# Two sets of row-wise Mamba blocks in one sequence of steps, and the layer's input added in the second

## The chip, the cores and the metric

The kernel runs on one core of a Trainium2 chip. The metric is device time in microseconds (us), from the first to the last instruction of one launch; lower is better. Eight runs of the kernel before gave 20162.97 to 20181.85 us, median 20176.18.

## What is computed

Four layers follow each other on a batch of four images of 48 x 48 pixels and 192 channels (the kernel holds an image as channels x 2304 pixels). Layers 0 to 2 are not touched by the change. Layer 3 normalizes its input `x`, runs a bidirectional Mamba block along each column of pixels (weights `mv`) and another along each row (weights `mh`), joins them with a linear layer, adds the input, and ends with a normalized two-layer MLP:

```python
xn = _layernorm(x, ln1_g, ln1_b)
h = _mamba_bidir(xn.reshape(B * H, W, C), ph).reshape(B, H, W, 2 * C)
xv = jnp.swapaxes(xn, 1, 2).reshape(B * W, H, C)
v = jnp.swapaxes(_mamba_bidir(xv, pv).reshape(B, W, H, 2 * C), 1, 2)
u = jnp.concatenate([v, h], -1)
x = x + jnp.einsum('bhwe,oe->bhwo', u, fc_w) + fc_b
xn2 = _layernorm(x, ln2_g, ln2_b)
m = jax.nn.gelu(jnp.einsum('bhwc,ec->bhwe', xn2, mlp_w1) + mlp_b1, approximate=False)
return x + jnp.einsum('bhwc,oc->bhwo', m, mlp_w2) + mlp_b2
```

One `_mamba` projects its input to `xi` and `z` (384 channels each), convolves `xi` over 4 pixels of the line, derives from it a step width `dt` and 16 pairs of coefficients B and C per pixel, and scans along the line, for each channel and each of 16 states: `h = exp(dt * A) * h + dt * x * B`. The output is the sum over the states of `h * C`, plus `D * xc`, times `silu(z)`, projected back to 192 channels.

## The kernel before

All data are float32. Layer 3 is three calls at the end of `network`: `row_mambas` for `mv` on the turned images `xn_wh`, `row_mambas` for `mh` on `xn_hw`, and `mlp`. The linear layer that joins the directions is folded into the weights beforehand: for each direction `row_mambas` multiplies `wo` (the Mamba block's own output projection) with a part of `fc` on PE, twice three products with two operand pairs each (tile `fp`, L1375 to L1380), and ACT copies them to `outT`. What remains for the end is `x3 + fc_b + f[1] + turned(f[0])`, where `f[0]` and `f[1]` are the outputs of the two sets in DRAM and `x3` is the layer's input.

**Jobs and groups.** A job is one direction of one piece of 384 pixels (eight lines of 48). There are 4 images x 6 pieces x 2 directions = 48 jobs in a set; the two directions of a piece are a pair, and the second (the *twin*) shares the input `u`, its projection `xh` and the gate `z` with the first. In a job, three blocks of 128 channels (index i) and four groups of four states (index g) make 12 groups. `run_jobs` goes through all groups of all jobs, one step each, and writes out by hand, for each step, what goes to which engine:

- DVE: the product `inputs` = `du` x B (into PSUM), then the scan `h`, always in program order (class `InOrder`).
- ACT: the decays `a` = exp(dt A) of the group two steps ahead, the copies out of PSUM, and the Silu and Softplus of later jobs, in a fixed order.
- POOL: the product `h` x C of the step's group (`weigh`), and, by step, a gate `yt` x `z` (steps 2, 6, 10 of a job) or a product `dus` (steps 1, 5, 9) behind it, all in program order.
- PE: the sum over states by matmuls of `h` with the identity into `y` (`reduce`, one step later), and the projections and convolutions of the next job.
- SP: all DMAs. A scheduler of the framework sets their order. B and C go to DRAM (`bc`) and come back broadcast to all partitions (`bcb`, 1536 KB per group of states, five buffers).

The work of the next job is a list of *units* (a PE part and an ACT part with the steps in which they may be issued), handed out by `Stream`. `MambaJob.outputs` gives two more units, which project a finished pair's `yt` with `outT` into `o` in steps 7 and 9 of the next pair's first job; after the second the store `f<-o` is issued. When a set ends, `run_jobs` first drains the pipeline, and when one begins, it loads a first job, projects and convolves it, and forms its first decays, all before the first group.

**Weights.** `MambaWeights` (L817) loads `xpT`, `dtT`, `vec` and `inT` and forms `A`, `diagD` and `diag` on ACT and DVE. `row_mambas` makes it once for each set, in a pool that is released at the end of the set.

**The MLP** (`mlp`, L1393) first loads its weights, then `pre(b)` loads three whole images (`macc` from `x3`, two `mf` from `f`; 1728 KB each) and adds them on DVE: two `scalar_tensor_tensor` (L1429), each on 96 x 2304, and two `tensor_tensor` with a turned operand (L1433). Six pieces per image then go through nine software-pipelined stages: mean, center, square, variance, root, scale, affine, hidden, close. Three buffers differ in number: `macc` has two, each `mf` one.

Of the kernel before, what the change touches and what calls it, by code (L numbers as in the profile page):

```python
# [14 lines left out]
ALU = mybir.AluOpType  # L15
PSUM = bass.MemoryType.PSUM

B = 4
S = 48
L = S * S  # L20
# [13 lines left out]
def halves(d):  # L34

    return d.rearrange("(k p) l -> p k l", p=Q)
# [11 lines left out]
class InOrder:  # L48


    def __init__(self, tc, engine):
        self.tc, self.engine = tc, engine
# [235 lines left out]
class ScanJob:  # L288
# [2 lines left out]

    def __init__(self, k, pools, w, c0, rev, prev):
        self.k, self.pools, self.w, self.c0, self.rev, self.prev = k, pools, w, c0, rev, prev
        self.entry, self.tokens = pools.entry(rev)
        self.bcb = {}
        self.y = {}
        self.a = {}
        self.h = {}  # L300
        self.du = {}
# [191 lines left out]
class MambaJob(ScanJob):  # L493

    skips = True

    def __init__(self, k, pools, w, c0, rev, prev, src, dst, mirror=False, twin=None):  # L500
        super().__init__(k, pools, w, c0, rev, prev)
        self.src, self.dst, self.mirror, self.twin = src, dst, mirror, twin
        self.paired = False
        if twin is not None:
            twin.paired = True
# [35 lines left out]
    def units(self, last):  # L541
# [40 lines left out]

        if self.twin is not None:
            self.z = self.twin.z
            outputs = last.outputs((7, 7), (9, 9)) if last is not None else []
            bc, deltas = self.projections(lambda: self.xs, (3, 3), (5, 5))
            return [conv(0, 0, 0), conv(1, 1, 2), conv(2, 2, 2), bc, *deltas, *outputs]
        outputs = last.outputs((4, 4), (6, 6)) if last is not None else []
        bc, deltas = self.projections(lambda: self.xs, (5, 5), (7, 7))
        return [  # L590
            inner(0, 0, 0),
# [2 lines left out]
            *(conv(i, min(2 + i, 3), 3) for i in range(3)),  # L594
            *outputs[:1],
            bc,
            *outputs[1:],
            *deltas,
            gate(0, 9, 10),
            gate(1, 10, 10),  # L600
            gate(2, 10, 10),
# [15 lines left out]
    def outputs(self, *slots):  # L617
        k = self.k
        if self.paired:
            return []  # L620
        step = -1 if self.mirror else 1
        jobs = [self] if self.twin is None else [self.twin, self]

        def project(m, slots):
            def act(ps):
                if m == 0:
                    self.o = k.tile(self.pools.one, [Q, 2, CH], "o")
                k.copy(self.o[:, m, ::step], ps)
                if m == 1:
                    d0 = L - CH - self.c0 if self.mirror else self.c0  # L630
                    k.nc.sync.dma_start(halves(self.dst)[:, :, d0 : d0 + CH], self.o)

            return self.unit(
                slots,
                Q,
                lambda ps: (
                    ps,
                    [
                        (job.w.outT[:, i, m * Q : (m + 1) * Q], job.yt[:, i, :])
                        for job in jobs  # L640
                        for i in range(3)
                    ],
                ),
                act,
            )

        return [project(m, slots[m]) for m in range(2)]


class Stream:  # L650
# [62 lines left out]
def run_jobs(jobs, side=None):  # L713
# [29 lines left out]
    for t in range(len(groups) + gated):  # L743
# [6 lines left out]
        if at == per - ahead:  # L750
            stream.run(at - 1)
        if at == taken + 3 and n + 1 == len(jobs) and n:
            Stream(jobs[n - 1].outputs((0, 0), (0, 0))).run(per)
        if t < len(groups):
            job, i, g = groups[t]
            job.scan(i, g)
# [6 lines left out]
        if t < len(groups):  # L763
# [3 lines left out]
            job, i, g = groups[t]  # L767
            job.weigh(i, g)
        stream.run(at if at < per - 1 else per)
        if side is not None and t < len(groups):  # L770
            if at == taken + 1 and n:
                offer(jobs[n - 1])
            side.slot(at)
            side.end()
# [4 lines left out]
        if 0 <= t - behind < len(groups):  # L779
            job, i, g = groups[t - behind]  # L780
            job.reduce(i, g)
    Stream(jobs[-1].outputs((0, 0), (0, 0))).run(per)
    offer(jobs[-1])


# [31 lines left out]
class MambaWeights(Weights):  # L817
    def __init__(self, k, pool, inT, xpT, dtT, vec, tag):
        super().__init__(k, pool, 128, 12, xpT, dtT, vec, tag)
        nc = k.nc  # L820
        self.D = self.vec[:, :, 17:18]
        self.cb = self.vec[:, :, 18:19]
        self.diagD = k.tile(pool, [128, 3, 128], f"diagD{tag}")
# [2 lines left out]
                self.diagD[:, i, :], k.ident, self.D[:, i, :], None, ALU.mult  # L826
            )
        self.taps = vec.shape[1] - 19
        self.inT = k.tile(pool, [Q, 2, 768], f"inT{tag}")
        nc.sync.dma_start(self.inT, inT.rearrange("(k p) m -> p k m", p=Q))  # L830
        self.diag = k.tile(pool, [128, 3, self.taps, 128], f"diag{tag}")
        for i in range(3):
            for t in range(self.taps):
                nc.vector.tensor_scalar(
                    self.diag[:, i, t, :],
                    k.ident,
                    self.vec[:, i, 19 + t : 20 + t],
                    None,
                    ALU.mult,
                )  # L840


def mamba_pass(k, pools, w, rev, src, dst, mirror=False):
# [18 lines left out]
def mamba_pair(k, weights, srcs, outs, mirror):  # L862

    with ExitStack() as ctx:
        pool = ctx.enter_context(k.tc.tile_pool(name="w", bufs=1))
        ws = []
        for n, (inT, xpT, dtT, vec, outT) in enumerate(weights):
            w = MambaWeights(k, pool, inT, xpT, dtT, vec, f"_{n}")
            w.outT = k.tile(pool, [128, 3, C], f"outT_{n}")
            k.nc.sync.dma_start(w.outT, outT.rearrange("(k p) m -> p k m", p=128))  # L870
            ws.append(w)
# [485 lines left out]
    return begin  # L1357


def row_mambas(k, weights, fcT, srcs, outs):  # L1360


    with ExitStack() as ctx:
        pool = ctx.enter_context(k.tc.tile_pool(name="w", bufs=1))
        inT, xpT, dtT, vec, wout = weights
        w = MambaWeights(k, pool, inT, xpT, dtT, vec, "")
        ws = [w, copy(w)]
        wo = k.tile(pool, [Q, 2, 2 * C], "wo")
        k.nc.sync.dma_start(wo, wout.rearrange("(k p) m -> p k m", p=Q))
        fc = k.tile(pool, [Q, 2, 2, C], "fc")  # L1370
        for n in range(2):
            k.nc.sync.dma_start(fc[:, n, :, :], fcT[n].rearrange("(k p) m -> p k m", p=Q))

        outT = [k.tile(pool, [128, 3, C], f"outT_{n}") for n in range(2)]
        with k.tc.tile_pool(name="fp", bufs=2, space=PSUM) as fp:  # L1375
            for n in range(2):
                for i in range(3):
                    p = k.tile(fp, [128, C], "fp")
                    k.mm(p, [(wo[:, m, i * 128 : (i + 1) * 128], fc[:, n, m, :]) for m in range(2)])
                    k.copy(outT[n][:, i, :], p)  # L1380
        pools = ScanPools(k, ctx, 1, True)
        jobs = []
        for n in range(2):
            ws[n].outT = outT[n]
        for b in range(B):
            for c in range(NCH):
                of = None, srcs[b], outs[b]
                first = MambaJob(k, pools, ws[0], c * CH, False, *of)
                jobs += [first, MambaJob(k, pools, ws[1], c * CH, True, *of, twin=first)]
        run_jobs(jobs)  # L1390


def mlp(k, f, fcb, ln2, w1T, b1, w2T, b2, x3, out):  # L1393

    nc, tc = k.nc, k.tc

# [2 lines left out]
    with (  # L1399
# [3 lines left out]
        tc.tile_pool(name="fout", bufs=2, space=PSUM) as po,  # L1403
        tc.tile_pool(name="fl", bufs=3, space=PSUM) as lnps,
    ):
        w1 = k.tile(one, [Q, 2, 3 * C], "mw1")
        nc.sync.dma_start(w1, w1T.rearrange("(k p) m -> p k m", p=Q))
        w2 = k.tile(one, [128, len(blocks), C], "mw2")
# [4 lines left out]
            nc.sync.dma_start(b1t[:n, e : e + 1], b1[at].rearrange("(p v) -> p v", v=1))  # L1413
        b2t = k.tile(one, [Q, 2], "mb2")
        nc.sync.dma_start(b2t, b2.rearrange("(k p) -> p k", p=Q))
        nw = k.tile(one, [Q, 2, 3], "mnw")
        nc.sync.dma_start(nw[:, :, 0:2], ln2.rearrange("(k p) v -> p k v", p=Q))
        nc.sync.dma_start(nw[:, :, 2:3], fcb.rearrange("(k p v) -> p k v", p=Q, v=1))
        acc, xn, hid = {}, {}, {}

        def pre(b):
            acc[b] = k.tile(pool, [Q, 2, L], "macc")
            nc.sync.dma_start(acc[b], halves(x3[b]))
            y = []
            for n in (1, 0):
                y.append(k.tile(one, [Q, 2, L], f"mf{n}"))
                nc.sync.dma_start(y[-1], halves(f[n][b]))
            for m in range(2):
                nc.vector.scalar_tensor_tensor(  # L1429
                    acc[b][:, m, :], acc[b][:, m, :], nw[:, m, 2:3], y[0][:, m, :], ALU.add, ALU.add  # L1430
                )
            for m in range(2):
                nc.vector.tensor_tensor(  # L1433
                    square(acc[b][:, m, :]),
                    square(acc[b][:, m, :]),
                    flipped(y[1][:, m, :]),
                    ALU.add,
                )

        def chunk(b, c):  # L1440
            return acc[b][:, :, c * CH : (c + 1) * CH]
# [30 lines left out]
def network(tc, d, out):  # L1472
    with ExitStack() as ctx:
# [44 lines left out]


        f = [images("f") for _ in range(2)]  # L1520
        for n, (p, src) in enumerate((("mv", xn[1]), ("mh", xn[0]))):
            ws = tuple(d[f"L3_{p}_{v}"] for v in ("inT", "xpT", "dtT", "vec", "Wout"))
            fcT = [d["L3_fcT"][2 * n + i] for i in range(2)]
            row_mambas(k, ws, fcT, src, f[n])
        mlp(k, f, *(d[f"L3_{v}"] for v in ("fc_b", "ln2", "w1T", "b1", "w2T", "b2")), x3, out)

# [114 lines left out]
```

## Time and profile before

| | us |
|---|---|
| median of 8 runs | 20176.18 |
| the profiled execution | 20172.9 |
| its span, first to last instruction | 20171.1 |
| first set: first product to end of last scan | 13525.79 to 16582.52 |
| second set: the same | 16638.98 to 19699.61 |
| MLP: first matmul to last operation | 19754.33 to 20167.2 |

| engine | busy, us | share of the span |
|---|---|---|
| PE | 17590.7 | 87% |
| DVE | 18228.2 | 90% |
| ACT | 12814.8 | 64% |
| POOL | 14692.9 | 73% |

The profile names an instruction by engine, line and the tiles it writes and reads (`out<-in`). A line can be a helper's: L56 stands for all operations that `InOrder` passes on, L93 for ACT, L114 for matmuls, so groups are told apart by their tiles. In the lines of a timeline, the first two numbers are the start and the duration in us, `x` gives how many instructions are merged into the row, and brackets hold the engine's idle time before it and what ended it. `SPq` rows are DMA issues, not transfers. In a table of stretches, each row has the stretch, its length, then busy time and count for PE, weight loads (PEld), DVE, ACT and POOL, then the granted TensorE clock (1.00 is full), the DMA engines' mean share, and GB/s.

### The profile page before, as it was taken

How to read it: one execution, taken by the hardware profiler on the slowest of the kernel's cores; microseconds unless marked ns; L12 is line 12 of the kernel's file. 1: busy time of each engine (PE TensorE's matmuls, PEld its weight loads, DVE VectorE, ACT ScalarE, POOL GpSimd, SP SyncE). 2: the span in 40 equal slices, each digit the busy share in tenths (PEclk: the TensorE clock that was granted, in tenths of full speed). 3: DMA queues.
4: the chain of work that ended last, by engine and by line, in shares of the span. 5: the costliest groups of instructions: out<-in, count | busy, mean ns of one | idle time of the engine just before them, and what ended most of it. 6: DMA issues, size and time to landing. Idle time of an engine off the chain costs nothing.

```text
span 20171.1 us, 159086 instructions
## 1 busy us (share of the span) xinstructions
PE 17590.7 (87%) x48144; PEld 8291.9 (41%) x48144; DVE 18228.2 (90%) x7435; ACT 12814.8 (64%) x22448; POOL 14692.9 (73%) x10748
## 2 busy tenths in 40 slices
PE   8999996999997778888888888879998988989988
PEld 4444443444444322233333333334444444444444
DVE  8999997999998499999999999969999989999993
ACT  6666664666665366666666766656666656666663
POOL 7777775777777177888877878757777767777770
PEclk9999998999999889989999999989999999999999
DMA  3323334333333266666666666642322222222222
GB/s 115 108 104 110 108 110 116 111 111 105 107 107 110 74 129 142 139 148 146 141 146 144 141 139 134 144 112 106 106 106 106 103 94 104 103 105 106 104 103 59
DMA packets 476473, 2320.46 MB, mean 115 GB/s; under 512 B 74553, under 2 KB 313761, under 8 KB 315105
## 3 DMA queue, kind: packets, MB, share of 16 engines
q1 hardware_dynamic: 475616, 2310.29, 40.7%
q8 instruction: 386, 6.32, 0.1%
q14 instruction: 471, 3.85, 0.1%
HBM read 2110.68 MB, written 199.40 MB: 115 GB/s over the span
## 4 chain that ended last, share of the span: by engine, by line
POOL 37%; DVE 35%; issue 11%; PE 11%; ACT 3%; DMA 3%; SPq 0%; DVEq 0%; POOLq 0%; ACTq 0%
POOL h L56 29%; DVE h L56 22%; DVE inputs L56 11%; PE y L56 5%; PE ps L56 3%; POOL dus L56 3%; POOL state L56 2%; POOL yt L56 1%; PE vps L114 1%; DMA bcb<-bc 1%; ACT a L93 1%; POOL bcb L56 1%; PE mop L114 1%; PE mps L114 1%; DVE vxi L1030 1%
## 5 line engine op out<-in xcount | busy, mean ns | idle before, releaser
L56 POOL TENSOR_TENSOR h<-h,bcb 128x1536 f32<-128x1536 f32 x3456 | 11914.4, 3447 | 1764.7 <-DVE h L56 1490.0
L56 DVE TENSOR_TENSOR_SCAN h<-a,inputs 128x1540 f32<-128x1540 f32 (+1 forms) x3456 | 11610.4, 3359 | 449.1 <-ACT a L93 12.7
L93 ACT ACTIVATE a<-delta,A 128x384 f32<-128x384 f32 (+1 forms) x13824 | 7447.9, 604 | 3369.5 <-DVE h L56 3357.7
L56 PE MATMUL y<-h,ident 128*128 128x384 f32 x18432 | 6806.7, 517 | 583.5 <-POOL h L56 578.4
L56 DVE TENSOR_TENSOR inputs<-du,bcb 128x1540 f32<-128x1540 f32 (+1 forms) x3456 | 6115.4, 1770 | 560.0 <-ACT du L93 206.6
L56 PEld LDWEIGHTS y<-h,ident 128*128 128x128 f32 x18432 | 3622.7, 201 | 3625.0 <-POOL h L56 1096.4
L56 PE MATMUL y<-h,sum 128*64 128x384 f32 x9216 | 3683.6, 549 | 577.0 <-POOL h L56 471.5
L56 PEld LDWEIGHTS y<-h,sum 128*64 128x64 f32 x9216 | 1297.8, 151 | 2921.7 <-issue 1758.7
L56 POOL COPY state<-h 128x4 f32<-128x4 f32 x2304 | 434.0, 188 | 2384.2 <-DVE h L56 2365.9
L56 PE MATMUL ps<-xh,diag 128*128 128x384 f32 x4032 | 1419.0, 491 | 196.1 <-ACT xc L93 196.1
L56 PE MATMUL ps<-u,inT 96*128 96x384 f32 x3456 | 1261.4, 496 | 198.8 <-ACT z L93 133.6
L56 PE MATMUL ps<-bcd,dtT 12*128 12x384 f32 (+1 forms) x2304 | 1022.3, 551 | 383.4 <-ACT delta L93 379.3
L56 PEld LDWEIGHTS ps<-xh,diag 128*128 128x128 f32 x4032 | 750.8, 189 | 790.3 <-ACT xc L93 282.9
L93 ACT ACT_TABLE_LOAD x793 | 1017.4, 1283 | 13.9
L90 ACT ACT_TABLE_LOAD x785 | 1007.2, 1283 | 14.1 <-PEq L1633 0.7
L56 PEld LDWEIGHTS ps<-u,inT 96*128 96x128 f32 x3456 | 651.3, 192 | 711.6 <-ACT z L93 210.7
L93 ACT ACTIVATE delta<-ps,vec 128x384 f32<-128x384 f32 x1152 | 632.9, 579 | 327.4 <-PE ps L56 320.0
L56 PE MATMUL ps<-yt,outT 128*96 128x384 f32 x2304 | 789.5, 486 | 0.7 <-POOL yt L56 0.7
L56 PEld LDWEIGHTS ps<-bcd,dtT 12*128 12x128 f32 (+1 forms) x2304 | 384.1, 192 | 953.2 <-ACT delta L93 616.7
L56 POOL TENSOR_TENSOR dus<-delta,xc 128x384 f32<-128x384 f32 x576 | 575.6, 999 | 139.6 <-ACT delta L93 139.6
L93 ACT ACTIVATE du<-dus 128x384 f32<-128x384 f32 x1152 | 560.5, 487 | 158.6 <-DVE inputs L56 153.0
L56 POOL TENSOR_TENSOR dus<-delta,xs 128x384 f32<-128x384 f32 x576 | 575.1, 999 | 56.0 <-ACT delta L93 56.0
(132 smaller groups left out, 9310.0 us busy)
## 6 DMA issues: line engine op xcount, KB each, us to landing
bcb<-bc SPq DMA_DIRECT2D x384, 1540.0 KB
bcb<-bc SPq DMA_DIRECT2D x768, 770.0 KB
bcb<-bc SPq DMA_DIRECT2D x384, 1536.0 KB
y<-o SPq DMA_DIRECT2D x192, 288.0 KB
xs<-xi_wh SPq DMA_DIRECT2D x96, 288.0 KB
xs<-xi_hw SPq DMA_DIRECT2D x96, 288.0 KB
added<-y SPq DMA_DIRECT2D x96, 288.0 KB
xs<-x_wh SPq DMA_DIRECT2D x96, 288.0 KB
```

What stands on the lines that cost most here:

```text
L56: return lambda *a, **kw: self.tc.keep_in_program_order(op(*a, **kw))
L90: self.in_order(self.nc.scalar.preload_act_table_set(LOG_EXP))
L93: return self.in_order(self.nc.scalar.activation(out, in_, func, **kw))
L114: (engine or self.nc.tensor).matmul(out, lhsT, rhs, start=start and i == 0, stop=stop and i == n - 1)
L1030: nc.vector.scalar_tensor_tensor(acc, taps, v[:, i, 1 + t : 2 + t], acc, ALU.mult, ALU.add)
```

## The change

Both sets become one list of jobs, and one call of `run_jobs`. `row_mambas` takes a list of sets; it makes the weights of both at the start, and the folds of both, with `wo` and `fc` in a pool that is released after them. Only `inT` keeps one buffer for both sets: a new method `enter` loads it, for the first set at once, for the second in step 1 of the first set's last-but-one job (`extras`, run by `run_jobs` after the step's units). The jobs of the second set get `prior`, the image of `x3`: their `outputs` have two more units, in steps 10 and 11, without a PE part, which add a loaded piece of `x3` to `o` on POOL, and the store follows the second of these.

In `mlp`, `x3` is no longer loaded. `load(b)` fetches `f[0][b]` into `mf` and `f[1][b]` into `macc` by halves (864 KB each) and adds both and the bias in one `scalar_tensor_tensor` per half, with `f[0]` read turned. `load(0)` stands ahead of the weights, and `pre(b)` calls `load(b + 1)`. `mf` now has two buffers. In the other user of `MambaWeights`, `mamba_pair`, `enter` is called right after the weights are made.

```diff
 # MambaJob.units
-            outputs = last.outputs((7, 7), (9, 9)) if last is not None else []
+            outputs = last.outputs((7, 7), (9, 9), (10, 10), (11, 11)) if last is not None else []
 # MambaJob.outputs
+        def add(m):
+            k.g.tensor_tensor(self.o[:, m, :], self.o[:, m, :], prior[:, m, :], ALU.add)
+            if m == 1:
+                store()
...
-                if m == 1:
-                    d0 = L - CH - self.c0 if self.mirror else self.c0
-                    k.nc.sync.dma_start(halves(self.dst)[:, :, d0 : d0 + CH], self.o)
+                if m == 1 and self.prior is None:
+                    store()
...
+        if self.prior is not None:
+            prior = k.tile(self.pools.one, [Q, 2, CH], "prior")
+            k.nc.sync.dma_start(prior, halves(self.prior)[:, :, d0 : d0 + CH])
+            units += [(slots[2 + m], lambda: None, lambda m=m: add(m)) for m in range(2)]
 # run_jobs
+        if t < len(groups):
+            for slot, extra in jobs[n].extras:
+                if slot == at:
+                    extra()
 # MambaWeights
+    def enter(self, tag="inT"):
+        self.inT = self.k.tile(self.pool, [Q, 2, 768], tag)
+        self.k.nc.sync.dma_start(self.inT, self.in_src.rearrange("(k p) m -> p k m", p=Q))
 # row_mambas
+        for (there, back), (*_, srcs, outs, prior) in zip(pairs, sets):
+            if jobs:
+                jobs[-2].extras = [(1, there.enter)]
+            else:
+                there.enter()
+            for b in range(B):
+                for c in range(NCH):
+                    of = None, srcs[b], outs[b]
+                    last = prior[b] if prior is not None else None
+                    first = MambaJob(k, pools, there, c * CH, False, *of)
+                    jobs += [
+                        first,
+                        MambaJob(k, pools, back, c * CH, True, *of, twin=first, prior=last),
+                    ]
         run_jobs(jobs)
 # mlp
+        def load(b):
+            acc[b] = k.tile(pool, [Q, 2, L], "macc")
+            y = k.tile(pool, [Q, 2, L], "mf")
+            for m in range(2):
+                nc.sync.dma_start(y[:, m, :], f[0][b][m * Q : (m + 1) * Q, :])
+                nc.sync.dma_start(acc[b][:, m, :], f[1][b][m * Q : (m + 1) * Q, :])
+                nc.vector.scalar_tensor_tensor(
+                    square(acc[b][:, m, :]),
+                    square(acc[b][:, m, :]),
+                    nw[:, m, 2:3],
+                    flipped(y[:, m, :]),
+                    ALU.add,
+                    ALU.add,
+                )
+
+        load(0)
...
         def pre(b):
-            acc[b] = k.tile(pool, [Q, 2, L], "macc")
-            nc.sync.dma_start(acc[b], halves(x3[b]))
-            y = []
-            for n in (1, 0):
-                y.append(k.tile(one, [Q, 2, L], f"mf{n}"))
-                nc.sync.dma_start(y[-1], halves(f[n][b]))
...
+            if b + 1 < B:
+                load(b + 1)
```

In the SP queue of the changed program, as the scheduler orders it: at the start, `xpT`, `dtT` and `vec` of both sets, `wo` and `fc` of both, then `inT`. In each pair of the second set, four `bcb` fetches, the store of `f`, the load of `prior`, and the next `bc` (in the first set, as before, the store stands ahead of the fourth `bcb`). At the end, the last store of `f`, `w1`, the first image's four halves, the other weights, the second image's halves.

## The prediction

> **What bounds the kernel now.** I read the page's activity slices first, then the busy time of each engine in the three stretches that the change touches, then the order of events at their seams.
>
> ```profile
> DVE  8999997999998499999999999969999989999993
> POOL 7777775777777177888877878757777767777770
> 13525.80:16582.50 3056.70, 2742.57 (x7679) 1450.79 (x7678) 2949.67 (x1152) 1964.43 (x3386) 2276.81 (x1140) 0.94 0.29 104
> 16638.90:19699.60 3060.70, 2745.68 (x7679) 1453.49 (x7678) 2949.68 (x1152) 1964.94 (x3387) 2277.26 (x1140) 0.94 0.29 103
> 19754.30:20166.50 412.20, 402.76 (x1152) 184.79 (x1152) 138.46 (x156) 182.48 (x259) 0.00 (x0) 0.99 0.22 52
> ```
>
> The first two lines are two rows of the 40 slices; the others give busy time by stretch (PE, weight loads, DVE, ACT, POOL, then clock, DMA share, GB/s). The first two stretches are the two sets of layer 3 blocks, from the first DVE product to the last scan: DVE is busy 96% of each, POOL 74%, DMA 29%. So in the sets DVE decides, with 576 groups in 3056.7 and 3060.7 us, 5.31 us a group. The last stretch is the MLP: PE is busy 402.8 of 412.2 us and decides, DVE a third. Between the stretches lie seams in which neither bounds anything. The first, by the timeline of DVE:
>
> ```profile
> 16579.17 3.35 DVE L56 TENSOR_TENSOR_SCAN h<-a,inputs 128x1536 f32<-128x1536 f32 x1
> 16600.17 0.06 DVE L249 MEMSET ones<- 128x1 f32 x1 [17.65 <-DMA f<-o]
> ...
> 16638.98 1.77 DVE L56 TENSOR_TENSOR inputs<-du,bcb 128x1536 f32<-128x1536 f32 x1 [34.87 <-ACT du L93]
> ```
>
> The last scan of the first set ends at 16582.52 and the next product begins at 16638.98: 56.46 us, in which the first set drains (17.65 us idle, then weights), and the second loads weights, folds `outT`, projects, convolves and forms its first decays. The seam to the MLP, seen from PE:
>
> ```profile
> 19714.30 0.33 SPq L631 DMA_DIRECT2D f<-o  x1
> 19717.02 0.33 SPq L1407 DMA_DIRECT2D mw<-in_L_w1T  x1
> ...
> 19742.42 5.14 DVE L1429 SCALAR_TENSOR_TENSOR macc<-macc,mnw,mf 96x2304 f32<-96x2304 f32 x2 [42.81 <-DMA mf<-f]
> 19750.18 8.03 DVE L1433 TENSOR_TENSOR macc<-macc,mf 96x2304 f32<-96x2304 f32 x2 [2.61 <-DMA mf<-f]
> 19754.33 2.84 PE L114 MATMUL ln_ps<-macc,mean 96*96 96x384 f32 x4 [40.58 <-DVE macc L1433]
> 19758.27 2.88 PE L114 MATMUL ln_ps<-macc,mean 96*96 96x384 f32 x4 [1.09 <-DVE macc L1433]
> ```
>
> **1. The merged sequence removes the first seam.** The boundary becomes an ordinary pair of jobs: the new set's projections and convolutions run beside the old set's last scans, as every pair's do. All 56.4 us go from DVE's path. The one new load there, `inT` (576 KB), is issued ahead of the last pair's `u`; in the pair shown at 18041, `u` is issued 66 us before its projection runs on PE at 18107.7. Even behind the old buffer's last reader that is cover enough. If it weren't, the span from first projection to first product (16613.34 to 16638.98, 25.6 us) would stay. Gain 56.4, bounds 30.8 and 56.4.
>
> **2. The same work at the start of the first set.** The second set's weights and folds now stand before the first set.
>
> ```profile
> 13495.86 6.06 PE L114 MATMUL fp<-fc,wo 96*128 96x192 f32 x24 [37.15 <-DMA fc<-in_L_fcT]
> 13497.52 0.33 ACT L93 ACTIVATE outT<-fp 128x192 f32<-128x192 f32 x1 [7.30 <-PE fp L114]
> ```
>
> Five more DMAs are issued before `wo` at 0.4 to 0.5 us each, and `inT` moves behind them (-0.5): PE starts about 2 us later. Six more fold groups follow on PE; the six of before took 5.9 us, three at 1.28 and, once the clock was up, three at 0.65. Six warm ones cost 3.9, cold ones 7.7. `inT`, last in the queue, is issued near 13494.7 and isn't read before 13507. The second set's 15 `diag` scalings on DVE (3.1 us, from the rows at 16601) lie under the wait for `fc`. All else follows the folds in order, so nothing hides this: +6.3 us (2.2 + 4.1), bounds 5.6 and 10.
>
> **3. The added input.** Per pair of the second set: one 288 KB load, and two POOL adds of 96x384. This shape has a row in another stage:
>
> ```profile
> 13424.42 0.99 POOL L56 TENSOR_TENSOR nx<-nx,nrs 96x384 f32<-96x384 f32 x1 [56.77 <-ACT nrs L93]
> ```
>
> So 48 x 0.99 = 48 us of POOL, in a queue that idles a quarter of the stage. By place: the first add stands in step 10 behind the `h` product and ahead of the `yt` gate, the second behind `h` of step 11. In the pair at 18101, `h` (3.41 from start to next), gate (0.94) and memset (0.15) end at 18106.02, and DVE releases the next `h` at 18106.73; with the add POOL is ready at 18107.03, 0.3 us late. Step 11 then ends with its add, the `xh` and `a` memsets near 18112.0, when the next release is due at 18112.07. The lag is gone within one step. Queued behind the adds are the gate (its product is read 8 steps on), the memset of the decay buffer (scanned two steps on, 10 us) and `h` (four buffers, read by PE one step on). DVE waits for none of them at once: cost 0; without cover up to 48.
>
> On SP the store of `f` now waits for the second add, about 12 us later than at present, and the load of `prior` follows it. In the first set, one broadcast fetch `bcb` stands behind the store; in the second, all four stand ahead of it, and behind it only the next `bc` store, which waits for ACT's `bcd` another 26 us (18112 to 18138). `prior` has one buffer, but is asked for right after it was read and used some 20 steps later. Cost 0; 24 x 288 KB is 2% of the stage's traffic.
>
> *By the Trainium skill*, "GPSIMD Engine Reference", section 4.1, elementwise two-input work belongs on VectorE, since GpSimd is about 2x slower; the rows here agree (0.95 us for DVE's 96x768 `ln_xm`, 0.99 for half of it on POOL). Followed, it would put 48 x 0.47 = 23 us on the engine that bounds this stage; the sum below stays with POOL at 0.
>
> **4. The MLP's start.** The image's sum now needs two loads instead of three and two DVE passes instead of four, in halves of 864 KB. At present the two first 1728 KB loads take 18.1 us from the first issue (19724.35) to the first pass, the third 7.76 more; so 1728 KB are worth 10.3 us in front and 7.76 after. The last store is 1.1 us later (one add on POOL, the other is under PE): 19715.4. The image's load is issued as `mw` is now, 2.7 later: 19718.1. First halves land at 19728.4, second halves at 19736.2. The fused pass, with the turned operand, isn't in the trace: its neighbours are the unturned one (2.61) and the turned add (4.10), both of 96x2304; it can't well be worse than the two it replaces (6.7). I take 4.1, as the turned read sets the row's length: second half done at 19740.3 against 19758.2 (when PE's fourth wait ends). That is 18; 1 us off for `mw`, which shares the queue: gain 17, bounds 13 and 20. The other weights stand behind these loads, but `w1` is ahead of them and `w2` isn't needed before the eighth stage of the first chunk, 20 us on.
>
> **5. The MLP's other images.** PE waits for L1433 at three more places: 0.64 + 1.86, 1.30 + 1.19, 1.36 + 1.20 = 7.55 us. A burst of 13.3 us on DVE becomes two passes of 4.1, asked for earlier. I take 4, bounds 0 and 7.5. Fewer DVE cycles elsewhere are worth nothing: PE bounds.
>
> **Sum**, from the profiled execution (20172.9, its span 20171.1): -56.4 + 6.3 + 0 - 17 - 4 = -71.1, 20101.8. The median of the runs is 3.3 above the profiled one: 20105.
>
> **Rivals**, on the median's scale.
> - *The adds cost what they take.* If `h`'s 0.3 us lag doesn't end within a step, but POOL's extra 2 us of each pair reach DVE: +48, 20153. Against it: POOL's 26% idle and the four `h` buffers. For it: step 11 closes with under 0.1 us to spare.
> - *The seam stays in part.* A new wait (for `inT`, or the new set's first `delta`) takes its place: +25.6, 20131. Against: 66 us of cover.
> - *The MLP doesn't start earlier*, because the loads are bound by DMA or a later weight replaces them: +21, 20126. For it: the first image's and the weights' bytes share one queue, and each DMA waits for an earlier one's semaphore.
> - *Slower than before.* The store on SP waits for POOL, and the next `bc` and its fetches queue behind store and `prior`. From 26 us of lateness on, each further microsecond is lost in each of 24 pairs; from 29 us it eats the gain (71/24 = 3 us a pair); at 31, 20105 + 24 x 5 = 20225. It needs `prior` to land over 100 us late; nothing in a queue at 29% shows that.
>
> **Chances**: forecast 0.70 (its own range 20088 to 20118, from the bounds of 2, 4 and 5), MLP unchanged 0.08, seam in part 0.07, adds 0.10, slower 0.05. The range 20085 to 20136 takes in the first three and leaves out the last two. A change under 0.2%, about 40 us, can't be told from none here: forecast, MLP and seam are faster (0.85), the adds' case is within 0.2% (0.10), the last slower (0.05).
>
> **What would show it.** DVE: no gap above 1 us at the boundary of the sets. First product about 6 us later after the last norm than now. The second set's 576 groups at 5.31 us as before, POOL busier by 48 us. First `ln_ps` matmul of the MLP 17 us after the last `f` store (now 40), those of the second half 25 us after it (now 44). The fused pass near 4.1 us. I am wrong if the second set's pairs lengthen from 127.6 us, or if a wait for `u`, `inT` or `prior` appears.

## The result and the profile after

The changed kernel takes 20108.27 us (median of 10 runs, 20100.88 to 20120.72) against 20179.51 for the kernel before (28 runs in the same series, 20162.97 to 20187.67): a ratio of 0.9966, interval 0.9958 to 0.9974. The forecast was 20105.0, on the base of the eight runs shown there. The profiled execution has a span of 20100.9 us (20171.1 before). The page's slices and the busy time by stretch for the two sets, from the first DVE product to the last scan (PE, weight loads, DVE, ACT, POOL, then clock, DMA share, GB/s):

```profile
DVE  8999997999998499999999999969999999999993
...
POOL 7777775777777177877878878757777777777770
```

```profile
13525.80:16585.85 3060.05, 2760.74 (x7740) 1461.16 (x7739) 2949.70 (x1152) 1983.09 (x3416) 2278.33 (x1149) 0.94 0.30 105
16585.85:19645.00 3059.15, 2752.26 (x7716) 1457.26 (x7715) 2949.68 (x1152) 1961.26 (x3380) 2323.59 (x1189) 0.95 0.30 105
```

The 8 that stood for the seam in the 33rd slice of DVE's row is now a 9. DVE's busy time is 2949.7 in each set, as before; POOL has 45 us more in the second and DVE paid nothing. Where the sets meet, DVE's timeline now reads:

```profile
16582.44 3.35 DVE L56 TENSOR_TENSOR_SCAN h<-a,inputs 128x1536 f32<-128x1536 f32 x1
16585.88 1.77 DVE L56 TENSOR_TENSOR inputs<-du,bcb 128x1536 f32<-128x1536 f32 x1
```

The last scan of the first set ends at 16585.79 and the second set's first product starts 0.09 us later, where 56.46 us lay before. At the start of layer 3, PE now folds twelve times in one go:

```profile
13491.72 10.30 PE L114 MATMUL fp<-fc,wo 96*128 96x192 f32 x48 [36.99 <-DMA fc<-in_L_fcT]
```

The seam to the MLP, by the timelines of SP, DVE and PE:

```profile
19660.73 0.31 SPq L634 DMA_DIRECT2D f<-o  x1
19661.08 0.45 SPq L1476 DMA_DIRECT2D mw<-in_L_w1T  x1
19663.80 0.32 SPq L1463 DMA_DIRECT2D mf<-f  x1
...
19673.70 4.11 DVE L1465 SCALAR_TENSOR_TENSOR macc<-macc,mnw,mf 96x2304 f32<-96x2304 f32 x1 [28.73 <-DMA macc<-f]
...
19677.87 2.87 PE L114 MATMUL ln_ps<-macc,mean 96*96 96x384 f32 x4 [18.76 <-DVE macc L1465]
...
19680.77 4.11 DVE L1465 SCALAR_TENSOR_TENSOR macc<-macc,mnw,mf 96x2304 f32<-96x2304 f32 x1 [2.96 <-DMA macc<-f]
...
19684.94 2.87 PE L114 MATMUL ln_ps<-macc,mean 96*96 96x384 f32 x4 [4.19 <-DVE macc L1465]
```

The two fused passes take 4.11 us each, and the second half's matmul starts 24.2 us after the last store (44 before).

The two profiled spans, cut at the same places, account for the whole difference:

| stretch | before | after | difference | predicted |
|---|---|---|---|---|
| start to first `xpT` load of layer 3 (SP) | 13486.58 | 13482.56 | -4.0 | 0 |
| from there to the first DVE product | 39.21 | 43.32 | +4.1 | +6.3 |
| from there to the end of the last scan | 6173.82 | 6119.09 | -54.7 | -56.4 |
| from there to the MLP's second-half matmul | 58.66 | 39.97 | -18.7 | -17 |
| from there to the end | 412.9 | 415.9 | +3.1 | -4 |
| sum | 20171.1 | 20100.9 | -70.2 | -71.1 |

The first row is code that the change does not touch. The same point lies between 13482.35 and 13491.02 in the ten profiles of the experiments below, so these 4 us are spread between executions. The fourth row has a spread of its own: `e3`, `e6`, `e7` and `e7b` below have the same program at this seam, and there it takes 41.1 to 42.0 us, a gain of 16.7 to 17.6. Their last store is issued 17.2 to 17.5 us after the last scan (15.8 in after); PE's last sum `y` took 2.85 us in after and 4.54 in `e3`.

### The profile page after: what moved, and what is told of

Read it like the earlier page. It is cut to its first block, busy times and chain, and to the rows that moved or that the text cites. A ratio compares the mean times of both kernels' runs of the same rounds, so it can differ in the third digit from the quotient of the medians.

```text
span 20100.9 us, 159205 instructions
## 1 busy us (share of the span) xinstructions
PE 17554.7 (87%) x48144; PEld 8281.1 (41%) x48144; DVE 18210.7 (91%) x7426; ACT 12817.8 (64%) x22450; POOL 14736.7 (73%) x10796
## 3 DMA queue, kind: packets, MB, share of 16 engines
q8 instruction: 386, 6.32, 0.1%
## 4 chain that ended last, share of the span: by engine, by line
POOL 37%; DVE 34%; PE 12%; issue 11%; ACT 2%; DMA 2%; DVEq 0%; SPq 0%; POOLq 0%; ACTq 0%
POOL h L56 30%; DVE h L56 22%; DVE inputs L56 11%; PE y L56 5%; PE ps L56 3%; POOL dus L56 3%; POOL state L56 2%; POOL yt L56 1%; PE vps L114 1%; POOL bcb L56 1%; ACT a L93 1%; PE mop L114 1%; DMA bcb<-bc 1%; PE mps L114 1%; DVE vxi L1060 1%
## 5 line engine op out<-in xcount | busy, mean ns | idle before, releaser
L56 POOL TENSOR_TENSOR h<-h,bcb 128x1536 f32<-128x1536 f32 x3456 | 11913.7, 3447 | 1710.5 <-DVE h L56 1434.8
L56 DVE TENSOR_TENSOR_SCAN h<-a,inputs 128x1540 f32<-128x1540 f32 (+1 forms) x3456 | 11610.3, 3359 | 450.4 <-ACT a L93 11.0
L56 PE MATMUL y<-h,ident 128*128 128x384 f32 x18432 | 6786.5, 516 | 556.8 <-POOL h L56 551.8
L56 DVE TENSOR_TENSOR inputs<-du,bcb 128x1540 f32<-128x1540 f32 (+1 forms) x3456 | 6115.5, 1770 | 512.5 <-ACT du L93 156.3
L56 PEld LDWEIGHTS y<-h,ident 128*128 128x128 f32 x18432 | 3615.8, 201 | 3588.2 <-POOL h L56 1068.3
L56 PE MATMUL y<-h,sum 128*64 128x384 f32 x9216 | 3671.6, 548 | 594.4 <-POOL h L56 483.8
L56 PEld LDWEIGHTS y<-h,sum 128*64 128x64 f32 x9216 | 1297.9, 151 | 2922.3 <-issue 1767.9
L56 POOL COPY state<-h 128x4 f32<-128x4 f32 x2304 | 434.0, 188 | 2378.4 <-DVE h L56 2351.8
L56 PE MATMUL ps<-xh,diag 128*128 128x384 f32 x4032 | 1419.7, 491 | 199.1 <-ACT xc L93 199.1
L56 PE MATMUL ps<-u,inT 96*128 96x384 f32 x3456 | 1259.2, 495 | 202.2 <-ACT z L93 136.0
L56 PE MATMUL ps<-bcd,dtT 12*128 12x384 f32 (+1 forms) x2304 | 1022.7, 551 | 381.3 <-ACT delta L93 377.6
L56 PEld LDWEIGHTS ps<-xh,diag 128*128 128x128 f32 x4032 | 750.8, 189 | 793.7 <-ACT xc L93 286.6
L56 PEld LDWEIGHTS ps<-u,inT 96*128 96x128 f32 x3456 | 650.0, 191 | 713.5 <-ACT z L93 215.2
L56 PE MATMUL ps<-yt,outT 128*96 128x384 f32 x2304 | 789.6, 486 | 0.7 <-POOL yt L56 0.7
L56 PEld LDWEIGHTS ps<-bcd,dtT 12*128 12x128 f32 (+1 forms) x2304 | 383.5, 192 | 950.7 <-ACT delta L93 615.2
L56 POOL TENSOR_TENSOR dus<-delta,xc 128x384 f32<-128x384 f32 x576 | 575.4, 999 | 104.6 <-ACT delta L93 104.6
L56 POOL TENSOR_TENSOR dus<-delta,xs 128x384 f32<-128x384 f32 x576 | 574.8, 998 | 59.8 <-ACT delta L93 59.8
```

Of the source, the lines that this page charges most:

```text
L56: return lambda *a, **kw: self.tc.keep_in_program_order(op(*a, **kw))
```

## The experiments

Each median below is set against runs of the kernel before in its own series. Their medians lie between 20166.7 and 20179.51 us, so a few us between two edited kernels are read from the stretches of their profiles, not from their medians.

### The two halves of the change, each alone

`e1_merge_only` merges the sets and leaves the input to the MLP, which is that of the kernel before:

```diff
-                        (None, x3)[n],
+                        None,
```

`e2_two_calls` adds the input in the second set and uses the new MLP, but calls `row_mambas` with a list of one set, twice:

```diff
+        for n, p in enumerate(("mv", "mh")):
+            row_mambas(
+                k,
...
+                        (None, x3)[n],
```

> Both sets in one sequence, but no added input in the second set and the MLP as before. My theory (the gain is two seams, each worth what it shows alone): first product of the first set to end of the last scan about 6119 us (6173.8 before), 4 us more of folds at the start, the MLP's start and rest as before: about 50 us below the kernel before. Rival (the boundary keeps part of its wait, and the rest of the gain comes from elsewhere): 25 us or less. The 54.7 us between the sets must show as a gap of under 1 us on DVE at the boundary.

> The other half alone: two calls as before, each with its own weights, but the input added in the second set and the new MLP. My theory: the seam between the sets stays at 55 to 57 us, the second set takes 3060 us as before, the MLP starts 19 us earlier after the last scan and takes 3 us more from then on: about 16 us below the kernel before, and with the run that merges alone it adds up to 66, near the 71 measured. Rival (the adds on POOL cost DVE something that the merge hides): the second set is longer by up to 48 us and the run is slower than before.

Merging alone: 20123.16 us (10 runs), ratio 0.9977 (0.9967 to 0.9986) to 20169.29, which is -46. Adding alone: 20145.85 (11 runs), ratio 0.9988 (0.9979 to 0.9997), -23. The sum, -69.6, is that of the whole change (-71.2) within the intervals: no sign that the halves meet. In `e1` the two sets take 6118.6 us with the start at 43.2, as in after, and the MLP's first matmul still waits 40.94 us. In `e2` the seam is still there, on DVE's timeline:

```profile
16580.08 3.35 DVE L56 TENSOR_TENSOR_SCAN h<-a,inputs 128x1536 f32<-128x1536 f32 x1
...
16636.64 1.76 DVE L56 TENSOR_TENSOR inputs<-du,bcb 128x1536 f32<-128x1536 f32 x1 [23.67 <-ACT du L93]
```

That is 53.2 us from the end of one set to the first product of the next (56.5 before), while the MLP's second-half matmul comes 42.4 us after the last scan (58.7 before: 16.3 less, where 19 was expected). `e2` gained 7 us more than expected of it. 3.3 us are the shorter seam, which was to stay at 55 to 57: its first fold begins 0.7 us earlier after the last scan, and from there to the next set's first product the same 88 matmuls run at a higher granted clock, by the two kernels' stretches (before, then `e2`):

```profile
16606.19:16638.98 32.79, 31.88 (x88) 19.87 (x89) 0.00 (x0) 13.07 (x24) 1.20 (x4) 0.80 0.24 97
16606.40:16636.64 30.24, 29.32 (x88) 18.20 (x89) 0.48 (x4) 13.05 (x24) 1.20 (x4) 0.87 0.34 112
```

Some 4 to 5 more are short gaps on DVE that fell away, which the last experiments take up.

### The MLP's later images: three buffers for the sum

The step that missed has a visible candidate. `macc` has two buffers, so an image's load can only be issued after the last reader of the image two before it; PE then waits, once per image and longer at a time. And in after the granted clock is low right behind these waits (columns as above):

```profile
19812.00:19816.00 4.00, 2.62 (x9) 1.19 (x8) 4.00 (x2) 3.94 (x6) 0.00 (x0) 1.00 0.67 177
19816.00:19820.00 4.00, 4.00 (x8) 1.46 (x8) 4.00 (x2) 1.28 (x1) 0.00 (x0) 0.69 0.00 0
19820.00:19824.00 4.00, 4.00 (x12) 2.03 (x11) 3.62 (x6) 0.00 (x0) 0.00 (x0) 0.89 0.00 0
19824.00:19828.00 4.00, 4.00 (x13) 1.88 (x12) 0.85 (x2) 0.52 (x1) 0.00 (x0) 1.00 0.13 32
19920.00:19924.00 4.00, 4.00 (x8) 1.53 (x7) 4.00 (x3) 0.00 (x0) 0.00 (x0) 0.50 0.01 4
19924.00:19928.00 4.00, 4.00 (x10) 1.93 (x9) 2.10 (x4) 0.00 (x0) 0.00 (x0) 0.66 0.00 0
```

At a clock of 0.69 PE gets through 8 matmuls in a 4 us stretch in which it is busy all the time; at 1.00 it does 13. These are means over 4 us. The clock record of the trace has only 1.00 and 0.50 here, and cut at its edges the low pieces are 3.41 and 6.83 us long:

```profile
19817.49:19820.90 3.41, 3.41 (x6) 1.62 (x7) 3.41 (x3) 0.00 (x0) 0.00 (x0) 0.50 0.00 0
19919.89:19926.72 6.83, 6.83 (x12) 2.82 (x11) 5.15 (x4) 0.00 (x0) 0.00 (x0) 0.50 0.01 2
```

```diff
-            acc[b] = k.tile(pool, [Q, 2, L], "macc")
+            acc[b] = k.tile(pool, [Q, 2, L], "macc", 3)
```

> The changed kernel with three macc buffers instead of two, so that the third image's load waits for nothing. My theory (the MLP's later part lost because PE waits 1.4 and 2.0 us for a late load at the third and fourth image, and its clock then falls to half for some us): both waits go, the granted clock stays at 1.00, and the time from the second half's first matmul to the end falls from 416 to about 408 us; in all 7 to 9 us below the changed kernel, near 20100. Rival (the fused pass of 4.1 us is what holds PE up): the passes still stand in front of the norm's small DVE operations, and the stretch stays at 413 us or more.

Measured: 20099.13 us (5 runs), ratio 0.9965 (0.9952 to 0.9977) to 20169.29. The stretch from the second-half matmul to the end is 407.3 us, 8.6 less than in after. The median does not show it: it is 70.2 us below its own series' before, after 71.2. PE's waits at the third and fourth image are gone, and the same stretch of this kernel, where the third image's sum is taken, keeps its clock:

```profile
19812.00:19816.00 4.00, 4.00 (x13) 1.64 (x12) 0.92 (x1) 2.42 (x5) 0.00 (x0) 1.00 0.97 221
19816.00:19820.00 4.00, 4.00 (x13) 1.66 (x12) 4.00 (x3) 3.94 (x5) 0.00 (x0) 1.00 0.42 122
```

So the account closes. In after PE waits 1.38 and 1.97 us at these two places (3.35), and the half clock costs 3.41 / 2 = 1.7 us behind the first and 6.83 / 2 = 3.4 behind the second: 8.5 of the 8.6 us between 415.9 and 407.3.

### How much POOL could take

Two kernels add more work of the same kind to POOL: each of the 48 adds gets two (`e4`) or six (`e4b`, EXTRA = 6) further adds ahead of it, into a spare tile that nobody reads. A helper's L56 is L57 in them.

```diff
+            for _ in range(EXTRA):
+                k.g.tensor_tensor(self.spare, self.o[:, m, :], prior[:, m, :], ALU.add)
             k.g.tensor_tensor(self.o[:, m, :], self.o[:, m, :], prior[:, m, :], ALU.add)
```

> The changed kernel with two more POOL adds of the same size beside each add (results unused, written to a spare tile): 96 more, four per pair of the second set, 96 us of POOL. My theory (POOL's idle quarter and the four h buffers cover a lag of a few us): the second set stays at 3059 us within 5, and the time within 10 us of the changed kernel. Rival (in this part of the pair POOL has no room, DVE pays what is added): the second set takes up to 96 us longer, 20205.

> After, with six more adds of the same size into a spare tile beside each of the 48 (288 more on POOL, 12 in each pair instead of 4 with the three-fold). Theory (POOL lags by what the adds take beyond its slack, and DVE waits only when the lag reaches the distance at which a buffer of h is wanted again): 14 adds of 1 us in a pair of 128 us are a lag of about 12 us at the step where they stand together, some 2 us beyond two steps of 5.33 us; DVE waits a few us in each of the 24 pairs, so 20 to 150 us slower than after. If DVE still does not wait, cover is over 12 us and the time is that of after within 10 us. Rival (POOL's work costs by its sum): 288 us slower, 20396 us.

With 96 more adds: 20104.94 us (6 runs), ratio 0.9969 (0.9957 to 0.998). The sets take 6109.9 us, 9 less than in after, with 21 short gaps on DVE fewer (about 8 us; see the last experiments), so DVE paid nothing for the adds there. Only behind the last scan, where nothing covers the last pair's adds, do they show: the last store is issued 19.6 us after it (15.8 in after). POOL's timeline in after shows why its own 48 cost nothing:

```profile
18050.25 1.00 POOL L56 TENSOR_TENSOR o<-o,prior 96x384 f32<-96x384 f32 x1
18051.21 1.00 POOL L56 TENSOR_TENSOR yt<-yt,z 128x384 f32<-128x384 f32 x1
18052.14 0.16 POOL L56 MEMSET a<- 128x32 f32 x1
18052.22 3.46 POOL L56 TENSOR_TENSOR h<-h,bcb 128x1536 f32<-128x1536 f32 x1
18055.63 1.01 POOL L56 TENSOR_TENSOR o<-o,prior 96x384 f32<-96x384 f32 x1
...
18057.48 3.45 POOL L56 TENSOR_TENSOR h<-h,bcb 128x1536 f32<-128x1536 f32 x1 [0.44 <-DVE h L56]
```

Behind the first add, POOL takes up the next `h` with no idle time: it is late. After the second it waits 0.44 us for DVE's scan again: the lag has lasted one step. With three times the adds it works back to back from 18046.21 to 18076.16, through six products of `h`, and DVE still waits for nothing.

With 288 more: 20271.3 us (4 runs), ratio 1.0047 (1.0031 to 1.0062), 163 us above after's median and not the 288 that the adds take. DVE's timeline has two waits in a pair of jobs, and POOL's shows the memset that the first waits for:

```profile
18143.18 3.35 DVE L57 TENSOR_TENSOR_SCAN h<-a,inputs 128x1536 f32<-128x1536 f32 x1 [5.42 <-POOL a L57]
18165.66 3.35 DVE L57 TENSOR_TENSOR_SCAN h<-a,inputs 128x1536 f32<-128x1536 f32 x1 [1.40 <-ACT a L94]
```

```profile
18135.32 6.35 POOL L57 TENSOR_TENSOR spare<-o,prior 96x384 f32<-96x384 f32 x6
18141.74 0.99 POOL L57 TENSOR_TENSOR o<-o,prior 96x384 f32<-96x384 f32 x1
...
18143.00 0.15 POOL L57 MEMSET a<- 128x32 f32 x1
```

The second set has 45 such waits, 164.6 us in all: 5.1 to 5.4 us at the first place, 1.2 to 2.7 at the second. It is 155 us longer than in after, and the MLP starts 12 us later behind the last scan, where the last pair's adds stand uncovered. What is late first is not `h` but the small memset of a decay buffer that stands behind the adds in POOL's program order; the scan two steps on needs that buffer. Twelve extra adds a pair cost about 7 us of waits and four cost none, so the cover beyond what after uses is some 5 to 6.6 us a pair (an estimate: 12 less 7, or less the first wait of 5.4).

### The adds on DVE

```diff
-            k.g.tensor_tensor(self.o[:, m, :], self.o[:, m, :], prior[:, m, :], ALU.add)
+            k.v.tensor_tensor(self.o[:, m, :], self.o[:, m, :], prior[:, m, :], ALU.add)
```

> After, with the 48 adds of the second set (o + prior, 96x384) on DVE instead of POOL. Theory (DVE bounds the layer, 96% busy in it, and POOL had the room): 48 adds of 0.48 to 0.52 us each stretch the second set by 23 to 25 us, so 20131 to 20134 us against 20108 for after; the set's time on DVE from its first product to its last scan goes from 3059 to 3082 or more. Rival (the order of the steps leaves DVE gaps that an add of half a microsecond falls into, or POOL's adds cost DVE as much through waits): within 5 us of after. DVE's idle of 0.48 us at single instructions, seen 22 times in the two sets of after and once in the kernel with three times the adds, can move either result by up to 8 us.

Measured: 20122.56 us (8 runs), ratio 0.9974 (0.9964 to 0.9984): 14 us above after's median, and 20 when each is taken against its own series' before (51.5 and 71.2 us faster). That is between the theory's 23 to 25 and the rival's 5. The sets take 6128.3 us, 9 more than in after, with eight short gaps fewer (about 3 us): 12 us for the adds. Another 3.4 us lie in the MLP's last stretch (419.3 us), where PE waits 2.29 us for `ln_rs`. So DVE pays, as the theory has it, but only 0.3 us for a row of 0.53, as the rival's reason has it:

```profile
16776.59 0.53 DVE L56 TENSOR_TENSOR o<-o,prior 96x384 f32<-96x384 f32 x1
16777.04 1.76 DVE L56 TENSOR_TENSOR inputs<-du,bcb 128x1536 f32<-128x1536 f32 x1
...
16782.65 1.75 DVE L56 TENSOR_TENSOR inputs<-du,bcb 128x1536 f32<-128x1536 f32 x1
```

The add's row starts 0.08 us before the scan ahead of it has ended and ends 0.08 into the product behind, and part of it fills what was a gap: from product to product it is 5.61 us, against 5.31 without an add. 48 x 0.30 = 14, near those 12. The Trainium skill's rule that the prediction quotes ("GPSIMD Engine Reference", section 4.1) has its durations right here (0.53 against 0.99 us), and following it would have cost some 12 us of the gain.

### The place of `inT` at the start

```diff
             pairs.append((w, copy(w)))
+            if s == 0:
+                w.enter()
...
-            else:
-                there.enter()
```

> After, with the 576 KB load of the first set's inT issued ahead of the loads of wo and fc, as in the kernel before, instead of behind them. Theory (after's first fold was not late although twelve weights and the second set's parameters came ahead of it, because the big load no longer stood in front of wo and fc): the first fold begins 11 to 12 us after the first xpT load is issued, against 9.2 in after, and the first product of the set comes 44.5 to 46 us after that load, against 43.3. Rival (the place of inT does not matter, the second set's small loads are what was overlapped): 43.0 to 43.6 again. Time of the whole kernel within 5 us of after.

One run, 20109.39 us. Its timelines:

```profile
13485.80 0.41 SPq L821 DMA_DIRECT2D xpT<-in_L_mv_xpT  x1
13496.72 10.95 PE L114 MATMUL fp<-fc,wo 96*128 96x192 f32 x48 [38.79 <-DMA fc<-in_L_fcT]
13531.53 1.77 DVE L56 TENSOR_TENSOR inputs<-du,bcb 128x1536 f32<-128x1536 f32 x1 [23.68 <-ACT du L93]
```

The first fold begins 10.92 us after the first `xpT` load (9.16 in after, 9.28 before), just short of the 11 to 12 expected, and the first product comes at 45.73 us (43.32, 39.21). In the nine profiles that fold twelve times with `inT` behind, the two lie at 9.0 to 9.4 and 43.2 to 43.7. With `inT` ahead the start would have cost 45.73 - 39.21 = 6.5 us; behind the small loads it cost 4.1. The theory holds. `e2`, which has one set's small loads with `inT` behind them, agrees: its first fold begins at 6.32 us, 3 earlier than before. Its first product comes no earlier (39.32), as its six folds took 7.50 us and not 6.06.

### Short gaps on DVE

The account above hides something. In after, DVE's timeline has a wait of 0.46 to 0.50 us at 22 single instructions of the two sets, such as these:

```profile
13768.69 3.35 DVE L56 TENSOR_TENSOR_SCAN h<-a,inputs 128x1536 f32<-128x1536 f32 x1 [0.48 <-ACT a L93]
18009.72 1.77 DVE L56 TENSOR_TENSOR inputs<-du,bcb 128x1536 f32<-128x1536 f32 x1 [0.46 <-DVE h L56]
```

Elsewhere the gap is 0.13 or less, but for 1.71 ahead of the first scan. They lie 61, 62, 123 or 184 instructions apart, about 163, 326 or 488 us, and the releasers named are simply the last ones. Before has 13 of them (1 in the first set, 12 in the second), after, `e1`, `e3` and `e6` have the same 22, `e5` 14, and `e2`, `e4` and `e4b` one. Two more kernels shift streams, both with three buffers of `macc`, by repeating the memset of the two mean weights ten times each, on DVE (`e7_shift_dve`, shown) or on POOL (`e7b_shift_pool`); one puts `e4` and three buffers together (`e8_x3_three_macc`).

```diff
         self.nc.vector.memset(w, 1.0 / n)
+        for _ in range(10):
+            self.nc.vector.memset(w, 1.0 / n)
```

> After with three buffers of macc, and 20 repeated memsets (96x96, about 0.1 us each) on DVE at the start of the program, which shift every later instruction of DVE's stream and change nothing else. Theory A (the single idle of 0.48 us on DVE, 22 times in the two sets of after, at distances that are multiples of about 162.8 us or 61 to 62 instructions, belongs to where the code lies): the number of such gaps in the two sets changes from 22, to few or none at best, and the two sets then take 6110 to 6112 us from the first product to the last scan against 6119 in after; the kernel takes 20091 us, against 20099 with three buffers alone. Theory B (the gaps belong to the work, say to a collision of buffers in the sequence of steps): 22 gaps at the same instructions of the two sets, and 20099 to 20101 us.

> After with three buffers of macc, and 20 repeated memsets (96x96) on POOL instead of DVE at the start of the program; DVE's stream is that of after. Theory A (the idle of 0.48 us belongs to the place of an instruction in DVE's own stream, as the shift of the gaps by DVE's memsets suggests): 22 gaps in the two sets, at the instructions at which after has them (the first at the 17th and the 79th of the set). Theory B (the place depends on what lies on the other engines as well, as the kernel with three times the adds and one gap suggests): another number of gaps, or other places.

> Both edits: three buffers of macc and the two extra adds into a spare tile beside each of the 48 (their work is thrown away; only the layout with few gaps of 0.48 us is wanted from them). If the gaps and the lost clock are separate costs that add: the two sets take 6110 us (6119 in after) with at most two gaps, the stretch from the second half's matmul to the end 407 to 409 us (416 in after), and the kernel 20089 to 20093 us against 20099 with three buffers alone. If the gaps' 8 us are made up elsewhere: 20097 us or more.

`e7_shift_dve`: 20100.05 us (5 runs), ratio 0.9964 (0.9952 to 0.9977), no gain. It has 21 gaps at other instructions (the first at the 82nd and 144th from the first product on, where after has the 30th and 92nd; the expectation of `e7b` counts these two from a later row), and the sets take 6117.3 us. So the gaps do not belong to the work; they move with DVE's stream. But their number stayed, against the expectation. `e7b_shift_pool` (one run, 20096.51 us): 22 gaps at after's places. `e8`: 20090.1 us (5 runs, 20089.2 to 20093.14), ratio 0.9962 (0.9949 to 0.9976) to 20166.7, with one gap; the sets take 6110.6 us, 8.5 less than in after, as expected. The MLP's last stretch is 410.1, a little over the 409 expected, with a wait of 2.58 us for `ln_rs` in it. It is the lowest median and ratio of all, though 96 adds in it are thrown away and its interval overlaps the others.

The DMA record of the traces narrows down what the gaps are. By the page, one queue carries instructions in pieces of 8 KB (`q14 instruction`; here from 13769.3 to 13769.5 us of after, 0.7 us behind the first line above: packets, MB, share):

```profile
q14 instruction: 1, 0.01, 17.2%
```

Such a piece starts 0.65 to 4.2 us after the end of every one of the 162 gaps in the twelve traces (0.66 to 0.72 us at 15 of after's 22), and that soon behind only 7 to 8% of DVE's other instructions. So the gaps stand where new instructions are fetched. A fetch alone does not make one: in `e4` a piece starts 1.06 us after the 30th and after the 92nd instruction has begun, and neither has a gap. What makes the gaps vanish in `e2`, `e4`, `e4b` and `e8` is open: DVE issues as many instructions in `e4` as in after.

## Why the prediction was right, and where it was not

1. **The first seam.** -54.7 us instead of -56.4. All of the seam went, none came back as a wait for `inT`, `u` or a first decay (0.09 us at the boundary, and `e1` alone gave it). The 1.7 us that lack are covered by nine more short gaps: 9 x 0.38 us (0.48 less an ordinary gap of about 0.1) = 3.4. Their count differs from program to program (1 to 22) though DVE's products and scans are the same, and the prediction had taken the sets' lengths (3056.7 and 3060.7) as fixed.
2. **The start of the first set.** +4.1 instead of +6.3. The twelve folds took 4.2 us more than six, as reckoned (4.1). The term that was wrong is the 2.2 us by which PE was to start later: it started 0.1 earlier. The prediction credited the move of `inT` with the 0.5 us of its issue; `e6` shows that the place of these 576 KB, behind the small loads or ahead of them, is worth 1.8 us of fold start and 2.4 us at the first product (0.65 of it slower folds, 10.95 us against 10.30).
3. **The added input.** 0, as predicted, and by the mechanism named. The 0.3 us lag appeared and was gone in one step, with 0.44 us to spare where under 0.1 was forecast. The rival that prices the adds at what they take is refuted by `e4`, as long as scans follow that cover them; `e4b` shows where the cover ends, and that it is the decay buffer's memset, which the prediction had listed with 10 us of cover, that decides. SP does wait for POOL's second add (131.9 us over 22 times, 6.0 at most), and no fetch was late for it; of the slower rival's 26 us it is a quarter.
4. **The MLP's start.** -18.7 instead of -17, inside the bounds, by the steps named: 17.1 and 24.2 us after the store (17 and 25 forecast), a pass of 4.11 (4.1). In the four other profiles with this seam the gain is 16.7 to 17.6, so the 1.7 beyond the forecast are spread.
5. **The MLP's other images.** +3.1 instead of -4: this step failed, and its bounds (0 to a gain of 7.5) did not hold the answer. It counted PE's waits alone. Those from the second half on did shrink, from 7.55 to 1.12 + 1.08 + 1.38 + 1.97 = 5.55 us. But before, they came in pairs, 0.64 + 1.86, 1.30 + 1.19 and 1.36 + 1.20, and the clock stayed at 1.00 through them; in after the third and fourth image have one wait each, and behind it PE ran at 0.50 for 3.41 and 6.83 us, worth 5.1 us: -2.0 + 5.1 = +3.1. `e3` shows both go with the third buffer. The cause of the longer wait is in step 5's own text: "asked for earlier" was not true for these images, whose load waits for a buffer (the third image's two halves of `macc` are issued at 19805.54, and DVE then stood 6.00 us for the first).

The errors partly cancel: 2.2 (step 2) and 1.7 us (step 4) more gain than reckoned, 1.7 (step 1) and 7.1 (step 5) less, 4.9 less on balance. By the rows of the account the change is worth 66.2 us, where the prediction had 71.1 and the medians give 71.2; the interval of the ratio (52 to 85 us) cannot tell these apart, and it is luck that the last two agree to 0.1. The forecast's own range, 20088 to 20118, is also wider than its reason: the bounds of steps 2, 4 and 5 give 20097.8 to 20116.7 around 20105. The measured 20108.27 lies in both.

## What to carry to other kernels

A seam between two passes that share their steps is worth what the bounding engine idles in it, if the next pass's loads fit the slack of the last one's. Work for an engine that trails the bounding one is free up to a lag that can be counted in steps; look for the first thing in its queue that the bounding engine reads, however small. When waits of PE are moved or merged, price them with the clock behind them (here one wait in place of two cost more than the two), and see whether one more buffer takes them away.

## What the runs showed that was not expected

- PE's granted clock fell to 0.50 after short idle times, which step 5 had not reckoned with: after 1.38 us for 3.41 us, after 1.97 us for 6.83 us, and in `e2` after a single 1.21 us (0.90, then 0.67, as means over 4 us). In before, waits of 0.64 and 1.86 us and of 1.30 and 1.19 us left it at 1.00, and so did 1.98 and 0.64 us in `e4b`. So the length of a wait alone does not tell. In the twelve traces, behind the MLP's second-half matmul, each of 13 waits of 1.2 us or more that stand alone was followed by 0.50, and none of eight pairs of 0.6 us or more that end 4.0 to 4.5 us apart was. The Trainium skill, "TensorE: Matmul & The Clock Gate", sections "What's actually happening" and "Why this matters for your kernels", gives half speed after an idle window of about 3.4 us, counted by a clock of its own, and warns of gaps over 3 us. The half speed agrees with the 0.50, and the length of the window with the low pieces of 3.41 us; that gaps under 2 us can bring it on is not what the warning says, and the measurement decides. Why a pair is spared stays open.
- The short gaps on DVE move with its instruction stream and are worth up to 8.5 us in 6119, more than the error of any step here. They stand where instructions are fetched; why some fetches stop DVE and others do not is open.
- A DVE add of 0.53 us between a scan and a product lengthened the step by 0.30 us in the rows shown.
